# Left halves of the adjacency cast by GpSimd's transfers, the attention row spread by TensorE, ScalarE's table loaded first, and new ranks, in a two-layer graph kernel

## The chip, the core and the metric

The kernel runs on one core of a Trainium2 chip. The core has five engines that run their own instruction streams in program order: TensorE (PE, matrix products into PSUM), VectorE (DVE), ScalarE (ACT), GpSimd (POOL) and SyncE (SP). SP, ACT and POOL also issue transfers; 16 DMA engines carry them. The metric is the device time of the program in microseconds, as the median of several runs.

## The reference

There are 16 graphs of 1024 nodes with 128 features, `x`, and one 0/1 adjacency matrix `adj` of 1024 x 1024 for all of them. Layer 0 is an attention layer, layer 1 a gated graph network of five steps; each is followed by a residual sum and a layer norm.

```python
# layer 0
h = x @ others_weight
u1, u2 = h @ a1, h @ a2                      # att_weight, two halves of 128
e = u1[:, idx1] + u2[:, idx2]                # idx1, idx2: fixed pairs (2m, 2m+1) mod n
e = where(e >= 0, e, 0.1 * e)
att = softmax(where(adj > 0, e, -9e15), axis=1)
x = layernorm(x + att @ h + x @ self_weight)
# layer 1
for _ in range(5):
    m = adj @ h                              # used twice: in_matrix = out_matrix = adj
    av = concatenate([m, m])
    u3 = h @ u3_w.T + u3_b
    z = sigmoid(av @ w3_w.T + w3_b + u3)
    r = sigmoid(av @ w4_w.T + w4_b + u3)
    hv = tanh(av @ w5_w.T + w5_b + (r * h) @ u5_w.T + u5_b)
    h = (1 - z) * h + z * hv
x = layernorm(x + h)
```

Because of the fixed pairs, the logits of the left 512 columns of `adj` depend on a pair of neighbouring nodes only, and those of the right 512 columns on the row alone. So the kernel treats the two halves of `adj` apart: for the left half it needs weighted row sums (the softmax's denominators), for the right half a plain count of ones in each row.

## The kernel before

**Tables.** `adj` (transposed by the host) is kept in SBUF for the whole run as `adj`, eight chunks c of 128 rows by 1024 columns, of type float32r, the type of the message products. float32 comes from memory, and a conversion has to write the float32r: the transfers land in staging tiles (`staged[k][e]`, chunk pair k = 0 to 3, e = 0 the left 512 columns, e = 1 the right), and `adj_tables` converts. The right halves go through ScalarE, which counts the ones as it copies (L497, `cnt`). The left halves are plain copies (L494), by VectorE for c < 4 and by ScalarE for the rest.

**Order.** All work is handed to `Plan` as operations with an engine, an assumed length in ns, a rank (lower is more urgent), and what they read and write. `Plan.order()` runs a list schedule over these assumed lengths and emits each engine's instructions in the order that comes out. On the chip the engines keep that order and wait on semaphores for the data. `rank_of(b, s)` gives graph b's step s its rank, from `D["q"]`, `D["s"]` and a correction in `NUDGE`; the constants of `D` shift single kinds of operation (`r`, `hv`, `tr`, `pr` of the gates, `l1` to `l8` the parts of layer 0, with own values for graphs 0 and 1). `lands(...)` are made-up operations on an engine "DMA" which tell the plan when a load is thought to arrive.

**The first microseconds.** `early_loads` (L347) issues, from SP and ACT by turns: graph 0's `x` in two halves, `others_weight`, the attention weights copied to all 128 partitions by the transfer itself (L351), the eight staged pieces of `adj`, `self_weight`, and graph 1's `x`. `ahead` (L461) then has SP load further graphs' `x` (L468). `constants` (L400, GpSimd) writes the identity matrix `ident` and the small tiles `shift`, `ones` and `mhalf`. `late_loads` (L378) makes GpSimd wait for the last staged piece before it issues the gates' weights.

TensorE begins with two `fill_` matmuls of the identity (L440) and then, wherever the plan finds no useful work for it, up to `IDLE` = 60 pairs of idle transposes of the identity (L436); nothing reads their results. Meanwhile VectorE's `wv_` (L412) multiplies `others_weight` by the two halves of the attention row, and sums (L414, L423). The result, in `T_ws` and `wo`, is what TensorE needs for graph 0's `spread_` (L767: the logit row of graph 0, spread to all partitions) and for the products `ph` (L690).

Graph 0's exponentials follow on VectorE and ScalarE (L770 to L783, into `pb`), then eight row sums `z_` (L855, VectorE), one for each chunk's left half, which for graph 0 read the staging tile; the reciprocals `rz_` (L874 to L878); the split of the scaled `h` into a high and a low float32r half, `hi_` on ScalarE (L907) and `lo_` on VectorE (L913); and the products `po` with `adj` (L648, with `po`). From there on TensorE works on several graphs at once: layer 0 of later graphs (`ph`, `po`, `px`) fits between the steps of layer 1, whose messages are the other products of L648 and whose gates are L1234, L1244, L1260 and L1261. The products `px` of graphs 4 to 7 (L472) can be done at any time and have a rank just before the idle transposes.

Of the kernel before, what the change touches and what calls it, by code (L numbers as in the profile page):

```python
# [17 lines left out]
P = 128  # L18
# [17 lines left out]
IDLE = 60  # L36
NUDGE = {(3, 2): -0.6, (3, 3): 0.3, (0, 1): -0.5, (1, 1): 0.45, (2, 3): -0.2, (3, 1): -1.2, (3, 0): 0.6, (0, 2): 0.25, (2, 2): -0.6, (1, 4): -1.2, (1, 3): 0.3, (0, 3): -0.6, (1, 2): -0.15, (4, 0): -0.1, (2, 0): 1.2, (2, 1): 0.05, (4, 4): -0.3, (2, 4): -0.15, (7, 3): -0.75, (5, 4): 1.2, (4, 3): 1.25, (6, 3): -1.5, (6, 4): -0.6, (8, 2): 0.15, 10: 0.05, (11, 3): -1.2, (11, 4): 0.3, (7, 2): 0.3, (8, 3): -0.6, (12, 3): -0.45, (13, 3): -0.9, (12, 0): 1.15, (10, 3): -0.35, (8, 4): 0.05, (12, 4): -0.3, (12, 1): -0.05, (11, 2): -0.15, 12: -0.05, (13, 4): 1.2, (13, 0): 1.2, (11, 1): 0.05, (12, 2): 0.15, (10, 4): 0.1, (15, 0): -0.6, (14, 2): -0.6}
# [106 lines left out]
def kernel(  # L144
# [79 lines left out]
    def exact(pools):  # L224
# [84 lines left out]
        D = dict(m=-0.05, pu=1.4, u=0.95, pr=0.55, pz=0.85, r=0.25, pv=1.05, z=1.3, hv=-0.7, h=1.2, tr=2.55, o=6.35, ln=2.5, out=4.4, l1=-9, l2=-4, l3=-2, l4=-5.5, l5=-7.25)  # L309
        D.update(l6=-1.35, l7=-1, l8=-2, q=10, s=4.2, even=1, base=-1, q1=-6, b1=4, lz=-4, l1_0=-9, l2_0=-4, lz_0=-4, l3_0=-2, l4_0=-4, l5_0=-7, l6_0=-1.5, l7_0=-1, l8_0=-2)  # L310
        D.update(l1_1=-10, l2_1=-9, lz_1=-4, l3_1=-2, l4_1=-4, l5_1=-7, l6_1=-1.5, l7_1=-1, l8_1=-2, tab=8, tabc=1, cl=-5.9, ca=-50, cr=-51, px=-3.5, own=-2, ownw=-4.6)

# [22 lines left out]
        def W(name):  # L335
            return T(boot)[:, cols[name]]

        ws = ("T", "ws")
        staged = [[("blk", "boot", k, e) for e in range(2)] for k in range(NC // 2)]
        x0 = ("xt", 0)  # L340

        def adj_half(k, e):
            hs = slice(e * HALF, (e + 1) * HALF)
            rows = adj_t[2 * k * P : 2 * (k + 1) * P, hs].rearrange("(c p) n -> p c n", p=P)
            return T(staged[k][e], F32, [P, 2, HALF]), rows

        def early_loads():  # L347
            nc.sync.dma_start(T(x0)[:, HALF:N], x_t[0][:, HALF:N])
            nc.scalar.dma_start(T(x0)[:, 0:HALF], x_t[0][:, 0:HALF])
            nc.sync.dma_start(wo[:, 0:P], others_w)  # L350
            nc.scalar.dma_start(T(ws)[:, P : 3 * P], att_w.rearrange("k o -> o k").to_broadcast([P, 2 * P]))  # L351
            nc.sync.dma_start(*adj_half(0, 0))
            nc.scalar.dma_start(*adj_half(1, 0))
            nc.sync.dma_start(*adj_half(0, 1))
            nc.scalar.dma_start(*adj_half(1, 1))
            nc.sync.dma_start(W("ws"), self_w)
            for k in range(2, NC // 2):
                for e in range(2):
                    nc.sync.dma_start(*adj_half(k, e))
            nc.sync.dma_start(T(("xt", 1)), x_t[1])  # L360
# [5 lines left out]
            writes=[(boot, "early"), (ws, "early"), (x0, "early"), (("xt", 1), "early"), *((t, "early") for k in staged for t in k)],  # L366
# [5 lines left out]
        lands(4700, [(x0, 0), (x0, 1)])  # L372
        lands(400, [(("wo",), 0), (ws, "att")])
        for ns, k, e in ((3600, 0, 0), (1400, 1, 0), (1000, 0, 1), (1400, 1, 1), (1600, 2, 0), (1400, 2, 1), (1400, 3, 0), (1400, 3, 1)):
            lands(ns, [(staged[k][e], 0), *([(boot, "ws")] if (k, e) == (2, 0) else [])])
        lands(1400, [(("xt", 1), 0), (("xt", 1), 1)])

        def late_loads():  # L378
            nc.gpsimd.tensor_copy(mark, T(staged[3][1])[0:1, 0, 0:1])
# [15 lines left out]
            reads=[(staged[3][1], 0)],  # L395
# [4 lines left out]
        def constants():  # L400
            make_identity(nc, ident)
            nc.gpsimd.memset(shift, -SHIFT)
            nc.gpsimd.memset(ones, 1.0)
            nc.gpsimd.memset(mhalf, -0.5)

        plan.add("POOL", 1400, -100, constants, writes=[(("ident",), 0), (("ones",), 0)])


        def column_(t, cols, n):
            nc.tensor.transpose(T(t)[:, 0:n], T(ws)[0:n, cols], ident[0:n, 0:n])  # L410

        def wv_():  # L412
            for two in range(2):
# [4 lines left out]
                    T(ws)[:, (1 + two) * P : (2 + two) * P],  # L418
# [12 lines left out]
        dve(650, -101, wv_, reads=[(ws, "att"), (("wo",), 0)], writes=[(ws, 0), (("look", "wv"), 0)])  # L431
# [58 lines left out]
        def adj_tables(c):  # L490
            st = staged[c // 2]

            def left(copy):
                copy(adj[:, c, 0:HALF], T(st[0])[:, c % 2])  # L494

            def right():
                nc.scalar.activation(adj[:, c, HALF:N], T(st[1])[:, c % 2], AF.Identity, accum_out=cnt[:, c : c + 1])  # L497

            if c < 4:
                dve(420, D["cl"], lambda: left(nc.vector.tensor_copy), reads=[(st[0], 0)], writes=[(("A",), c, 0)])  # L500
            else:
                act(A, D["ca"], lambda: left(nc.scalar.copy), reads=[(st[0], 0)], writes=[(("A",), c, 0)])
            act(640, D["cr"], right, reads=[(st[1], 0)], writes=[(("A",), c, 1)])

        def quarter(i, j):
# [1235 lines left out]
```

## Time and profile before

| | |
|---|---|
| Median of 9 runs | 1455.59 us (1453.86 to 1457.94) |
| Profiled execution, its own time | 1456.06 us |
| Its span, first to last instruction | 1454.5 us |
| Granted TensorE clock, mean over the span | 0.996 |
| Instructions | 17779 |
| Idle transposes (L436) | 120, 14.3 us busy |
| Fill matmuls (L440) | 4 passes, 3.7 us busy |
| Left-half casts (L494) | 4 on VectorE, 1.6 us; 4 on ScalarE, 2.4 us |
| Right-half copies (L497) | 8, 5.0 us, and 1.8 us for reading their sums |
| DMA of the span | 174.28 MB, mean 120 GB/s |

The span is the time from the first to the last instruction of one profiled execution; the program's own time lies 1.6 us above it. Busy shares are of the span. TensorE's busy time counts idle transposes and fills too. The profile gives a float32 matmul as two passes (`x4` for two matmuls), and matmuls overlap, so that the length of one in a row is longer than the time from one to the next. In the timeline the lines "SPq", "ACTq" and "POOL ... DMA_DIRECT2D" are issues of transfers, the time that the issuing engine needs for them, not the transfers.

### The profile page before, as it was taken

The numbers are of one execution on the slowest core, as the hardware profiler recorded it, in microseconds if no ns is written. First come the engines' busy times: TensorE is split into PE (matmuls) and PEld (weight loads), VectorE is DVE, ScalarE is ACT, GpSimd is POOL, SyncE is SP. The second block draws the span as 40 slices with busy tenths as digits, with TensorE's granted clock in tenths as the row PEclk, the third lists the DMA queues.
The fourth block names the chain that finished last, engine by engine and source line by source line (L and its number), as shares of the span: only waits on it lengthen the run. The fifth ranks groups of instructions, "written<-read, shape, count | busy, mean of one in ns | idle before, by whom it ended". The sixth has DMA issues, their size and how long they took to land. (4 is left out here: it accounts for less than half of the span.)

```text
span 1454.5 us, 17779 instructions
## 1 busy us (share of the span) xinstructions
PE 1435.8 (99%) x5017; PEld 899.2 (62%) x5017; DVE 1160.3 (80%) x2752; ACT 898.2 (62%) x1793; POOL 192.1 (13%) x334
## 2 busy tenths in 40 slices
PE   9999999999999999999999999999999999999996
PEld 7666666566666666666656556666665666566562
DVE  6886989879888798888889698887988876865635
ACT  5665546656656766576656666566574766653644
POOL 1221001102010120111101121010210112000302
PEclk9999999999999999999999999999999999999998
DMA  8245135544344643364445543365423554223111
GB/s 289 89 132 148 56 109 164 156 136 125 83 135 129 178 136 102 97 179 130 117 114 147 152 124 81 103 172 161 120 76 94 153 160 113 75 66 87 37 37 32
DMA packets 187299, 174.28 MB, mean 120 GB/s; under 512 B 34408, under 2 KB 136504, under 8 KB 187192
## 3 DMA queue, kind: packets, MB, share of 16 engines
q1 hardware_dynamic: 180920, 155.23, 37.8%
q0 software_dynamic: 5168, 16.26, 3.4%
q10 hardware_dynamic: 1104, 1.57, 0.3%
q8 instruction: 41, 0.67, 0.2%
q14 instruction: 66, 0.54, 0.1%
HBM read 95.74 MB, written 77.24 MB: 119 GB/s over the span
## 5 line engine op out<-in xcount | busy, mean ns | idle before, releaser
L1261 PE MATMUL ps_g_v<-r,u5h 128*128 128x512 f32 x320 | 163.5, 592 | 0.5 <-DVE r L1254 0.5
L1260 PE MATMUL ps_g_v<-m,wm 128*128 128x512 f32 x320 | 163.4, 592 | 0.0
L1254 DVE SCALAR_TENSOR_TENSOR r<-r,hT 128x512 f32<-128x512 f32 x160 | 109.1, 686 | 64.0 <-ACT r L1247 63.2
L1244 PE MATMUL ps_g_r<-m,wm 128*128 128x512 f32 x320 | 159.1, 593 | 1.0 <-ACT gz L1237 1.0
L1244 PE MATMUL gz<-m,wm 128*128 128x512 f32 x320 | 158.1, 592 | 0.0
L1269 DVE TENSOR_TENSOR hv<-hv,hT 128x512 f32<-128x512 f32 x160 | 109.8, 686 | 55.2 <-ACT hv L1266 54.4
L1234 PE MATMUL ps_g_r<-hT,u 128*128 128x512 f32 x320 | 152.7, 592 | 0.0
L1247 ACT ACTIVATE r<-ps_g_r,bh 128x512 f32<-128x512 f32 x160 | 109.3, 686 | 64.4 <-PE ps_g_r L1244 63.7
L648 PE MATMUL ps_acc_a<-tab,blk_s 128*128 128x512 f32 x544 | 147.7, 413 | 0.0
L648 PE MATMUL ps_acc_po<-adj,blk 128*128 128x512 f32 x512 | 139.6, 418 | 0.1
L1237 ACT COPY gz<-ps_g_r 128x512 f32<-128x512 f32 x160 | 91.3, 572 | 63.2 <-PE ps_g_r L1234 61.8
L648 PEld LDWEIGHTS ps_acc_a<-tab,blk_s 128*128 128x128 f32 x544 | 101.1, 188 | 33.3 <-issue 8.1
L1247 ACT ACTIVATE z<-gz,bh 128x512 f32<-128x512 f32 x160 | 109.5, 687 | 17.7 <-PE gz L1244 17.2
L648 PEld LDWEIGHTS ps_acc_po<-adj,blk 128*128 128x128 f32 x512 | 95.8, 188 | 35.1 <-issue 11.5
L1275 DVE SCALAR_TENSOR_TENSOR hT<-hv,hT 128x512 f32<-128x512 f32 x160 | 108.4, 680 | 1.5
L1272 DVE SCALAR_TENSOR_TENSOR hv<-z,hv 128x512 f32<-128x512 f32 x160 | 108.3, 678 | 0.6
L1261 PEld LDWEIGHTS ps_g_v<-r,u5h 128*128 128x128 f32 x320 | 60.6, 190 | 77.5 <-issue 61.3
L1244 PEld LDWEIGHTS gz<-m,wm 128*128 128x128 f32 x320 | 60.3, 189 | 74.8 <-issue 74.3
L606 DVE STREAM_TRANSPOSE T<-hT 128x512 f32<-128x512 f32 x138 | 95.5, 700 | 3.9 <-DMA X<-T 3.2
L648 PE MATMUL ps_acc<-adj,blk_h 128*128 128x512 f32 x384 | 95.4, 402 | 1.0 <-ACT blk_h L636 0.8
L1260 PEld LDWEIGHTS ps_g_v<-m,wm 128*128 128x128 f32 x320 | 60.0, 190 | 57.6 <-issue 51.7
L640 DVE TENSOR_TENSOR blk_s<-G,blk_s 128x512 fp32r<-128x512 f32 x136 | 91.8, 680 | 2.9 <-ACT blk_s L636 2.7
(199 smaller groups left out, 2520.8 us busy)
## 6 DMA issues: line engine op xcount, KB each, us to landing
G<-X SPq DMA_DIRECT2D x140, 256.0 KB, 2.9
X<-T SPq DMA_DIRECT2D x552, 64.0 KB, 1.8
yd<-y POOLq DMA_DIRECT2D x32, 256.0 KB, 3.1
D_y<-T_y SPq DMA_DIRECT2D x112, 64.0 KB, 1.9
F_y<-D_y SPq DMA_DIRECT2D x28, 256.0 KB, 2.8
X<-y SPq DMA_DIRECT2D x28, 256.0 KB, 2.1
D_b<-T_b SPq DMA_DIRECT2D x112, 64.0 KB, 2.6
F_b<-D_b SPq DMA_DIRECT2D x28, 256.0 KB, 2.9
```

What stands on the lines that cost most here:

```text
L606: nc.vector.transpose(T(t).rearrange("p (b c i) -> p b c i", b=4, c=4), turned(src()))
L640: lambda: nc.vector.tensor_tensor(half(1), src(), half(0), ALU.subtract),
L648: nc.tensor.matmul(T(bank), T(blk)[:, k, c, :], right(c), start=(first and i == 0), stop=(last and i == len(terms) - 1), skip_group_check= ...
L1234: nc.tensor.matmul(T(pr), u3, h(), start=True, stop=True)
L1244: nc.tensor.matmul(T(p_), wm[:, j, :], T(m), start=False, stop=True, skip_group_check=True)
L1247: nc.scalar.activation(T(t), T(p_), AF.Tanh, bias=bh[:, j : j + 1], scale=0.5 * sg)
L1254: lambda r=r, h=h: nc.vector.scalar_tensor_tensor(T(r), T(r), 1.0, h(), ALU.add, ALU.mult),
L1260: nc.tensor.matmul(T(pv), wm[:, 2, :], T(m), start=True, stop=False)
L1261: nc.tensor.matmul(T(pv), u5h, T(r), start=False, stop=True)
L1269: nc.vector.tensor_tensor(T(hv), T(hv), h(), ALU.subtract)
L1272: nc.vector.scalar_tensor_tensor(T(hv), T(z), 1.0, T(hv), ALU.add, ALU.mult)
L1275: nc.vector.scalar_tensor_tensor(h(), T(hv), 0.5, h(), ALU.mult, ALU.add)
```

## The change

- `early_loads` no longer loads the left halves of `adj`; the staging tiles for them are gone. SP issues the four right halves; ACT issues only its half of `x` and the attention weights, now as one row on one partition.
- `constants` issues four transfers from GpSimd, one for each chunk pair, from `adj` in memory straight into the left half of the float32r table; the transfer converts. They stand after the memsets of `ones` and `shift`, and before the identity and `mhalf`. Its assumed length in the plan is 1400 ns, as before.
- The eight left-half copies of `adj_tables` are gone. The row sums `z_` of graph 0 read the table.
- `pw_` is a new TensorE operation: a matmul with a row of ones copies the attention row to all partitions, in PSUM, and `wv_` reads it there.
- `first_` is a new ScalarE operation at the head of its queue: an exponential of one element, which makes it the first operation to use ScalarE's table.
- The assumed arrivals (`lands`) are new, `IDLE` is 48, and a part of the ranks in `D` and `NUDGE` has other values.

```diff
--- before.py
+++ after.py
@@ -33,8 +33,8 @@
 AHEAD = range(4, 8)
 LATE = 3001
 TURNED = {(0, 0), (0, 1), (7, 2), (7, 3)}
-IDLE = 60
-NUDGE = {(3, 2): -0.6, (3, 3): 0.3, (0, 1): -0.5, (1, 1): 0.45, ...}
+IDLE = 48
+NUDGE = {(3, 2): -0.75, (3, 3): 0.75, (0, 1): -0.5, (1, 1): 1.05, ...}
 
 
 class Plan:
@@ -306,9 +306,9 @@
             plan.add("SP", *a, **k)
 
 
-        D = dict(m=-0.05, pu=1.4, u=0.95, pr=0.55, pz=0.85, r=0.25, pv=1.05, z=1.3, hv=-0.7, h=1.2, tr=2.55, o=6.35, ln=2.5, out=4.4, l1=-9, l2=-4, l3=-2, l4=-5.5, l5=-7.25)
-        D.update(l6=-1.35, l7=-1, l8=-2, q=10, s=4.2, even=1, base=-1, q1=-6, b1=4, lz=-4, l1_0=-9, l2_0=-4, lz_0=-4, l3_0=-2, l4_0=-4, l5_0=-7, l6_0=-1.5, l7_0=-1, l8_0=-2)
-        D.update(l1_1=-10, l2_1=-9, lz_1=-4, l3_1=-2, l4_1=-4, l5_1=-7, l6_1=-1.5, l7_1=-1, l8_1=-2, tab=8, tabc=1, cl=-5.9, ca=-50, cr=-51, px=-3.5, own=-2, ownw=-4.6)
+        D = dict(m=-0.05, pu=1.4, u=0.95, pr=0.75, pz=0.85, r=0.45, pv=1.05, z=1.3, hv=0.3, h=1.2, tr=2.35, o=6.35, ln=2.5, out=4.4, l1=-9, l2=-5, l3=-2, l4=-4.5, l5=-7.25)
+        D.update(l6=-1.35, l7=-2, l8=-2.4, q=10, s=4.2, even=1, base=-1, q1=-6, b1=4, lz=-5, l1_0=-7, l2_0=-4, lz_0=-4, l3_0=0, l4_0=-4, l5_0=-7, l6_0=-0.5, l7_0=-5, l8_0=-4)
+        D.update(l1_1=-12, l2_1=-8, lz_1=-3, l3_1=-2, l4_1=-6, l5_1=-7, l6_1=-2.5, l7_1=-2, l8_1=-2, tab=8, tabc=1.5, cl=-5.9, ca=-50, cr=-51, px=-4.0, own=-2, ownw=-4.6)
 
         def on_pe(b, what):
 
@@ -336,47 +336,45 @@
             return T(boot)[:, cols[name]]
 
         ws = ("T", "ws")
-        staged = [[("blk", "boot", k, e) for e in range(2)] for k in range(NC // 2)]
+        staged = [("blk", "boot", k) for k in range(NC // 2)]
         x0 = ("xt", 0)
 
-        def adj_half(k, e):
-            hs = slice(e * HALF, (e + 1) * HALF)
-            rows = adj_t[2 * k * P : 2 * (k + 1) * P, hs].rearrange("(c p) n -> p c n", p=P)
-            return T(staged[k][e], F32, [P, 2, HALF]), rows
+        def adj_rows(k, e):
+            return adj_t[2 * k * P : 2 * (k + 1) * P, e * HALF : (e + 1) * HALF].rearrange("(c p) n -> p c n", p=P)
+
+        def adj_half(k):
+            return T(staged[k], F32, [P, 2, HALF]), adj_rows(k, 1)
 
         def early_loads():
             nc.sync.dma_start(T(x0)[:, HALF:N], x_t[0][:, HALF:N])
             nc.scalar.dma_start(T(x0)[:, 0:HALF], x_t[0][:, 0:HALF])
+            nc.scalar.dma_start(T(ws)[0:1, P : 3 * P], att_w.rearrange("k o -> o k"))
             nc.sync.dma_start(wo[:, 0:P], others_w)
-            nc.scalar.dma_start(T(ws)[:, P : 3 * P], att_w.rearrange("k o -> o k").to_broadcast([P, 2 * P]))
-            nc.sync.dma_start(*adj_half(0, 0))
-            nc.scalar.dma_start(*adj_half(1, 0))
-            nc.sync.dma_start(*adj_half(0, 1))
-            nc.scalar.dma_start(*adj_half(1, 1))
-            nc.sync.dma_start(W("ws"), self_w)
-            for k in range(2, NC // 2):
-                for e in range(2):
-                    nc.sync.dma_start(*adj_half(k, e))
+            for k in range(NC // 2):
+                nc.sync.dma_start(*adj_half(k))
+                if k == 1:
+                    nc.sync.dma_start(W("ws"), self_w)
             nc.sync.dma_start(T(("xt", 1)), x_t[1])
 
         sp(
             9500,
             -103,
             early_loads,
-            writes=[(boot, "early"), (ws, "early"), (x0, "early"), (("xt", 1), "early"), *((t, "early") for k in staged for t in k)],
+            writes=[(boot, "early"), (ws, "early"), (x0, "early"), (("xt", 1), "early"), *((t, "early") for t in staged)],
         )
 
         def lands(ns, what):
             plan.add("DMA", ns, -103, lambda: None, writes=what, lag=0)
 
-        lands(4700, [(x0, 0), (x0, 1)])
-        lands(400, [(("wo",), 0), (ws, "att")])
-        for ns, k, e in ((3600, 0, 0), (1400, 1, 0), (1000, 0, 1), (1400, 1, 1), (1600, 2, 0), (1400, 2, 1), (1400, 3, 0), (1400, 3, 1)):
-            lands(ns, [(staged[k][e], 0), *([(boot, "ws")] if (k, e) == (2, 0) else [])])
+        lands(4650, [(x0, 0), (x0, 1), (ws, "att")])
+        lands(650, [(("wo",), 0)])
+        for ns, k, e in ((2000, 0, 0), (1400, 0, 1), (1400, 1, 0), (1400, 1, 1), (1600, 2, 0), (1400, 2, 1), (1400, 3, 0), (1400, 3, 1)):
+            landed = [(staged[k], 0)] if e else [(("A",), c, 0) for c in (2 * k, 2 * k + 1)]
+            lands(ns, landed + ([(boot, "ws")] if (k, e) == (2, 0) else []))
         lands(1400, [(("xt", 1), 0), (("xt", 1), 1)])
 
         def late_loads():
-            nc.gpsimd.tensor_copy(mark, T(staged[3][1])[0:1, 0, 0:1])
+            nc.gpsimd.tensor_copy(mark, T(staged[3])[0:1, 0, 0:1])
             for j, w in enumerate((w3_t, w4_t, w5_t)):
                 nc.gpsimd.dma_start(
                     W("w345")[:, 256 * j : 256 * (j + 1)].rearrange("p (t e) -> p t e", t=2),
@@ -392,22 +390,34 @@
             11000,
             -80,
             late_loads,
-            reads=[(staged[3][1], 0)],
+            reads=[(staged[3], 0)],
             writes=[(boot, "late"), (("uw",), 0), (ws, "b")],
             lag=2500,
         )
 
         def constants():
+            nc.gpsimd.memset(ones, 1.0)
+            nc.gpsimd.memset(shift, -SHIFT)
+            for k in range(NC // 2):
+                nc.gpsimd.dma_start(adj[:, 2 * k : 2 * k + 2, 0:HALF], adj_rows(k, 0))
             make_identity(nc, ident)
-            nc.gpsimd.memset(shift, -SHIFT)
-            nc.gpsimd.memset(ones, 1.0)
             nc.gpsimd.memset(mhalf, -0.5)
 
         plan.add("POOL", 1400, -100, constants, writes=[(("ident",), 0), (("ones",), 0)])
+
+        def first_():
+            nc.scalar.activation(mark, shift[0:1, :], AF.Exp)
+
+        act(1600, -104, first_, reads=[], writes=[(("mark",), 0)])
 
 
         def column_(t, cols, n):
             nc.tensor.transpose(T(t)[:, 0:n], T(ws)[0:n, cols], ident[0:n, 0:n])
+
+        pw = ("ps", "g", "w")
+
+        def pw_():
+            nc.tensor.matmul(T(pw)[:, 0 : 2 * P], ones[0:1, 0:1].to_broadcast([1, P]), T(ws)[0:1, P : 3 * P], start=True, stop=True)
 
         def wv_():
             for two in range(2):
@@ -415,7 +425,7 @@
                     T(("look", "wv"))[:, two * P : (two + 1) * P],
                     wo[:, 0:P],
                     1.0,
-                    T(ws)[:, (1 + two) * P : (2 + two) * P],
+                    T(pw)[:, two * P : (two + 1) * P],
                     ALU.mult,
                     ALU.mult,
                     accum_out=wv[:, two : two + 1],
@@ -428,7 +438,8 @@
             nc.vector.tensor_copy(wo[:, P : P + 2], wv)
             nc.vector.tensor_copy(wo[:, P + 2 : P + 3], T(ws)[:, 0:1])
 
-        dve(650, -101, wv_, reads=[(ws, "att"), (("wo",), 0)], writes=[(ws, 0), (("look", "wv"), 0)])
+        pe(450, -101, pw_, reads=[(ws, "att"), (("ones",), 0)], writes=[(pw, 0)])
+        dve(750, -101, wv_, reads=[(pw, 0), (("wo",), 0)], writes=[(ws, 0), (("look", "wv"), 0)], lag=-250)
         dve(190, -65, wo_, reads=[(ws, 0)], writes=[(("wo",), 1)])
 
         def idle_():
@@ -490,19 +501,10 @@
         def adj_tables(c):
             st = staged[c // 2]
 
-            def left(copy):
-                copy(adj[:, c, 0:HALF], T(st[0])[:, c % 2])
-
             def right():
-                nc.scalar.activation(adj[:, c, HALF:N], T(st[1])[:, c % 2], AF.Identity, accum_out=cnt[:, c : c + 1])
-
-            if c < 4:
-                dve(420, D["cl"], lambda: left(nc.vector.tensor_copy), reads=[(st[0], 0)], writes=[(("A",), c, 0)])
-            else:
-                act(A, D["ca"], lambda: left(nc.scalar.copy), reads=[(st[0], 0)], writes=[(("A",), c, 0)])
-            act(640, D["cr"], right, reads=[(st[1], 0)], writes=[(("A",), c, 1)])
-
-
+                nc.scalar.activation(adj[:, c, HALF:N], T(st)[:, c % 2], AF.Identity, accum_out=cnt[:, c : c + 1])
+
+            act(640, D["cr"], right, reads=[(st, 0)], writes=[(("A",), c, 1)])
 
         def quarter(i, j):
             return lambda c: adj[:, 4 * i + c, j * HALF : (j + 1) * HALF]
@@ -849,12 +851,10 @@
             rank = rank0(b) + lv("lz")
             for c in range(NC):
 
-                st = staged[c // 2][0]
-
-                def z_(c=c, st=st):
+                def z_(c=c):
                     nc.vector.scalar_tensor_tensor(
                         T(junk),
-                        T(st)[:, c % 2] if b == 0 else adj[:, c, 0:HALF].bitcast(F32),
+                        adj[:, c, 0:HALF].bitcast(F32),
                         1.0,
                         pairs()[:, c // 4, :],
                         ALU.mult,
@@ -862,7 +862,7 @@
                         accum_out=T(zs)[:, c : c + 1],
                     )
 
-                entries = (st, 0) if b == 0 else (("A",), c, 0)
+                entries = (("A",), c, 0)
                 dve(740, rank, z_, reads=[(pb, 0), (pb, 1), entries], writes=[(zs, c), (junk, 0)])
 
 
```

(`NUDGE` is cut: it also has new values for other steps of graphs 0 to 3, and three new entries; those of graphs 4 to 15 are unchanged.)

## The prediction

> **What bounds the kernel.** I read the page's busy shares first, then TensorE's waits, then the first 30 us of the timeline, then GpSimd's rows there.
>
> ```profile
> PE 1435.8 (99%) x5017; PEld 899.2 (62%) x5017; DVE 1160.3 (80%) x2752; ACT 898.2 (62%) x1793; POOL 192.1 (13%) x334
> ```
>
> TensorE is busy in all but 18.7 us of the 1454.5 us span. Its waits over the whole span (us in total, times, longest):
>
> ```profile
> PE ps_t L598 <- DVE hT L1275: 4.4, 2, 3.6
> PE gz_fill L440 <- POOL ones L403: 1.4, 1, 1.4
> PE ps_g_r L1244 <- ACT gz L1237: 1.0, 2, 0.7
> PE ps_acc L648 <- ACT blk_h L636: 0.8, 1, 0.8
> PE ps_g_v L1261 <- DVE r L1254: 0.5, 1, 0.5
> PE ps_acc L648 <- DVE blk_h L640: 0.2, 1, 0.2
> PE ps_t_b L598 <- ACT y L565: 0.2, 1, 0.2
> ```
>
> These are 8.5 us; the other 10 us lie behind the last transposes of the tail. In the middle TensorE goes from one useful matmul to the next, so it can't be shortened there. The change keeps every useful matmul and adds one. So I count TensorE's **waste**: the wait before its first matmul, the fills of L440, the idle transposes of L436, the waits. What the waste loses, the end gains, one for one. The head of the timeline holds most of it (start, length, engine, line, what; in brackets the idle time before it):
>
> ```profile
> 1.35 3.68 PE L440 MATMUL gz_fill<-ident 128*128 128x512 f32 x4 [1.35 <-POOL ones L403]
> 4.87 3.44 PE L436 MATMUL ps_idle<-ident 128*128 128x128 f32 x30
> 7.16 0.29 DVE L414 SCALAR_TENSOR_TENSOR look_wv<-wo,T_ws 128x128 f32<-128x128 f32 x1 [7.16 <-DMA T_ws<-in_L_gnn_att_weight_dram]
> 8.14 1.90 PE L767 MATMUL ps_p<-xt,T_ws 128*128 128x512 f32 x4
> 10.13 1.28 ACT L779 ACT_TABLE_LOAD   x1 [10.13 <-PE ps_p L767]
> 11.66 4.75 PE L436 MATMUL ps_idle<-ident 128*128 128x128 f32 x42
> ```
>
> TensorE runs in program order. The fills need the identity, cost 3.5 us (1.35 to 4.87: these first passes are slow, 0.86 us against the 0.43 of L767's), then idle transposes at 4.68/42 = 0.11 us each cover the wait for the attention row.
>
> **GpSimd's queue, the dear part.** `constants` now issues four casting transfers ahead of the identity. What one issue holds GpSimd for, from its rows:
>
> ```profile
> 1.29 0.10 POOL L403 MEMSET ones<- 128x2 f32 x1
> 19.86 2.41 POOL L381 DMA_DIRECT2D hT_boot<-in_L_gnn_w_w_dram  x3
> 22.26 0.58 POOL L385 DMA_DIRECT2D u<-in_L_gnn_u_w_dram  x1
> 26.56 0.49 POOL L388 DMA_DIRECT2D T_ws<-in_L_gnn_u_b_dram  x1 [1.71 <-DMA hT_boot<-in_L_gnn_w_w_dram]
> 44.64 0.66 POOL L1054 DMA_DIRECT2D yd<-y  x1 [2.86 <-ACT y L565]
> ```
>
> One row costs 0.49, 128 rows 0.58 (64 KB) or 0.66 (256 KB), 256 rows 0.80. No row casts. The new transfers have 256 rows of 2 KB, so the nearest is 0.80. Lower end 0.49; upper end 2.1, if the cast cuts each row into four pieces of 512 bytes (768 more rows, at 0.22 per 128, from the step 0.58 to 0.80). I take 0.80: 4 x 0.80 = 3.2 us. The identity (0.2 and 0.29) follows, so TensorE starts at about 4.6 instead of 1.35: **+3.2** (ends +2.0 and +8.4). Behind the transfers wait only the identity, mhalf, and the late loads, which waited until 19.73 for adj anyway. `ones` and `shift` go ahead, so the row's matmul and the table load don't wait for the transfers themselves; but in TensorE's queue the row's matmul stands behind fills and idle transposes, so it is late with them.
>
> The Trainium skill weighs against 0.80 here: "DMA: Bandwidth & Descriptors", on the anatomy of a DMA of the GpSimd path, puts the dispatch at about 50 ns and the making of descriptors at "small, variable". By it four issues would be some 0.2 us, an estimate, and the sum would end near -2.1 instead of +0.9; the 0.80 of this trace decides.
>
> **IDLE from 60 to 48**: 24 transposes fewer, 24 x 0.11 = **-2.7**. They have to be replaced by useful work, or TensorE merely waits in their place; that is a rival below.
>
> **The attention row**: one matmul of 256 columns, two passes at half of L767's 0.43: **+0.43**, with VectorE's sums behind it (some 0.2 us of draining; 0.9 for L414 and L423), which the idle transposes planned between them cover. The broadcast load goes. With it the first spread would be free of the 7.16, but TensorE now gets there later: start 4.6, fills to 8.1, about 14 transposes to 9.7, the row to 10.1, sums to 11.2. The spread stands at some 11.3 instead of 8.14. That the row lands early is worth nothing, hidden by TensorE's own queue.
>
> **Table load first**: 1.28 us leave the chain spread, exponentials, row sums, and go where ScalarE waited until 10.13. **Casts gone**: four of 0.42 on VectorE, four of 0.62 on ScalarE (2.5). ScalarE worked without pause from 10.13 to the first L907 at 23.79, 13.7 us; less 1.28 and 2.5 it is 9.9, from 11.3 + 2.0 = 13.3 to 23.2. VectorE's last reciprocals, before at 22.7, come at about 22.7 + 3.2 - 1.3 - 0.4 = 24.2. So the split halves for the first products are ready about when they were (24.2 against 23.8), while TensorE reaches them 0.9 late: no new wait, and no gain either. All of this costs and brings nothing on TensorE's count; without the slack it would cost the 0.4.
>
> **Transfers.** In us 4 to 6 the DMA engines moved 83 GB/s, in 6 to 20 385. Without the dip 2 x (385 - 83) = 0.6 MB come earlier, 1.6 us, so adj would be there at 18.1 rather than 19.7. Two fewer issues on ScalarE's queue, two fewer on SP's: each 0.4 to 0.5, all before either engine has other work, so nothing. Row sums now wait for the cast tile instead of the staged one; same landing. The cast's rate is in no row: bounds are the 385 of the plain loads and half of it (below).
>
> **New ranks**: best, all waits that aren't the last one of the tail go: 1.0 + 0.8 + 0.5 + 0.2 + 0.2 + 0.8 (4.4 - 3.6) = -3.5. Worst, each of the eight pairs gets a hole like that at 40 to 50 us, where TensorE was busy 8.8 of 10: +9.7. I take 0, since the middle is already full.
>
> **Sum**: 3.2 - 2.7 + 0.43 = **+0.9** on the profiled span of 1454.5. That execution took 1456.06, 0.5 over the median of 1455.59; I add to the median: **1456.5**.
>
> **Rivals.**
> B, the waits go: the new ranks and earlier loads take away all 3.5 us: 0.9 - 3.5 = -2.6, 1453.0; with issues at 0.49 it is 2.0 - 2.7 + 0.4 - 3.5 = -3.8, 1451.8. For it: fewer fillers are asked for. Against: TensorE starts later, and the waits near 46 to 50 follow a chain over GpSimd's row statistics that no edit shortens.
> C, the issues are dear (slower): place, GpSimd's first microseconds; price 4 x issue - 2.3; it decides from 1.3 us an issue, where the sum is +2.9. At 2.1 it is +6.1, 1461.7. For: no cast in the trace. Against: all three kinds of issue lie below 0.81.
> D, the casting transfers move at half rate (slower): 2.1 MB take 10.8 us instead of 5.4, adj is there at 23.5, 3.8 later than before, TensorE only 0.9 later; it stands 2.9, where the dropped transposes were: +3.8, 1459.4. It decides from about two thirds of the rate on.
> E, the ranks open holes in the middle: up to +9.7; two such holes, 2.4, make +3.3, 1458.9.
> That the change doesn't do what it says, casting elsewhere, I see no way to.
>
> **How the numbers follow.** What a measurement of this kernel can tell from no change is about 0.2%, 2.9 us: faster is below 1452.7, slower above 1458.5. Forecast 0.50 (its own range 1454.5 to 1459: issues of 0.7 to 1.0, a wait more or less; 0.03 of it slower), B 0.20 (0.18 faster, since it needs nearly all its waits or a cheap issue; 0.02 same), C 0.13, D 0.10, E 0.07. So faster 0.18, same 0.49, slower 0.33. The range 1452 to 1461 leaves out B's far part and the far parts of C and E.
>
> **What would show it.** GpSimd's four issues between the memsets and the identity, their length, and TensorE's first matmul at 4 to 5 us; the spread at 11 rather than 8; 96 idle transposes; the table load before 3.5 us; no casts at L494; waits of TensorE before 50 us no longer than before. An issue below 0.5 or above 1.3 us, a fresh wait of 2 us between 15 and 35 us, or holes in the middle would make me wrong.

## The result, and the profile after

The changed kernel takes 1461.52 us (median of 9 runs, 1458.68 to 1463.42), beside 1455.30 us for the kernel before on the same chip (29 runs, 1453.71 to 1457.94). The ratio is 1.004, interval 1.0032 to 1.0048: 6.2 us slower, where +0.9 was forecast and 1461 was the upper end. The profiled execution took 1459.51 us, its span is 1457.7 us, 3.2 more than before; it is one of the quicker of its kind, so only half of the loss can be read in it. A further 0.25 of the loss lies outside the span: the program's own time is 1.56 above it before and 1.81 after.

Busy time and instruction counts of the page, and TensorE's waits (us in total, times, longest):

```profile
PE 1434.1 (98%) x4995; PEld 897.7 (62%) x4995; DVE 1158.6 (79%) x2748; ACT 898.3 (62%) x1790; POOL 210.2 (14%) x338
```

```profile
PE gz_fill L451 <- POOL mhalf L404: 5.0, 1, 5.0
PE ps_t L600 <- DVE hT L1275: 4.4, 2, 3.6
PE ps_acc_a L650 <- ACT m L1186: 1.9, 1, 1.9
PE ps_g_r L1244 <- ACT gz L1237: 1.2, 1, 1.2
PE ps_acc_c L650 <- DVE blk_s L642: 0.8, 1, 0.8
PE ps_acc L650 <- DVE blk_h L642: 0.5, 1, 0.5
```

TensorE has 22 passes fewer (24 idle transposes less, two passes of the row more). The wait at the end of the tail is the same 3.6. The wait for the identity grew from 1.4 to 5.0. And there are new rows in the middle: single waits of up to 1.9 us on products there, where the largest was 0.8.

The head of the timeline (start, length, engine, line, what; in brackets the idle time before it):

```profile
1.31 3.10 POOL L402 DMA_DIRECT2D adj<-in_adj_dram  x4 [0.45 <-issue]
1.76 1.28 ACT L409 ACT_TABLE_LOAD   x1 [1.76 <-issue]
...
5.05 3.48 PE L451 MATMUL gz_fill<-ident 128*128 128x512 f32 x4 [5.05 <-POOL mhalf L404]
8.36 1.69 PE L447 MATMUL ps_idle<-ident 128*128 128x128 f32 x14
9.98 0.69 PE L420 MATMUL ps_g_w<-T_ws,ones 1*128 1x256 f32 x2
10.71 0.29 DVE L424 SCALAR_TENSOR_TENSOR look_wv<-wo,ps_g_w 128x128 f32<-128x128 f32 x1 [10.71 <-PE ps_g_w L420]
11.75 1.88 PE L769 MATMUL ps_p<-xt,T_ws 128*128 128x512 f32 x4
```

Four issues hold GpSimd from 1.31 to 4.41, 0.775 us each. The identity follows, and TensorE's first matmul is at 5.05. The row's matmul, its sums and the spread come as a chain behind that.

The middle has the new part. First the timeline near 360 us, then TensorE, TensorE's weight loads, VectorE, ScalarE and GpSimd in stretches of 2 us (busy us and instructions of each, then granted clock, DMA share, GB/s):

```profile
358.52 0.34 SPq L626 DMA_DIRECT2D G<-X  x1
359.04 1.50 PE L692 MATMUL ps_g_ph<-wo,xt 128*128 128x131 f32 x12
361.28 0.62 ACT L638 CAST blk_x<-G 128x512 fp32r<-128x512 f32 x1 [4.50 <-DMA G<-X]
361.80 0.58 ACT L1186 COPY m<-ps_acc_a 128x512 f32<-128x512 f32 x1
362.44 3.26 PE L650 MATMUL ps_acc_a<-tab,blk_s 128*128 128x512 f32 x8 [1.89 <-ACT m L1186]
```

```profile
360.00:362.00 2.00, 0.55 (x5) 0.35 (x4) 0.07 (x1) 0.72 (x2) 0.00 (x0) 1.00 0.84 256
362.00:364.00 2.00, 1.56 (x5) 1.28 (x6) 2.00 (x5) 1.22 (x4) 0.00 (x0) 0.77 0.44 118
364.00:366.00 2.00, 2.00 (x7) 1.61 (x7) 1.65 (x4) 0.26 (x1) 0.00 (x0) 0.50 0.20 51
366.00:368.00 2.00, 2.00 (x9) 1.39 (x9) 1.64 (x9) 1.22 (x3) 0.00 (x0) 0.88 0.63 107
```

In ScalarE's program the cast of a message block (L638) stands ahead of the copy that frees TensorE's accumulator (L1186). The cast waits for a transfer that was issued at 358.52; ScalarE stands idle for 4.50 us, and the copy, whose input had been there since about 359.2, stands behind it. TensorE waits 1.89 us for the copy, then runs for 3.41 us at half the clock (363.07 to 366.49 in the records), which loses about 1.7 more.

Summing, over the whole span, the gaps between the starts of successive matmuls beyond their regular step (worked out from the two traces), together with what the granted clock did at the start and at the end, gives this account of the profiled 3.2 us:

| | before | after | difference, us |
|---|---|---|---|
| wait for the first matmul | 1.35 | 5.05 | +3.7 |
| idle transposes | 120 | 96 | -2.6 |
| the fills, at half speed | 3.5 us | 3.3 us | -0.2 |
| the row's matmul | | | +0.5 |
| holes behind the head, half clock included | about 5 | about 7 | about +2 |
| the tail: the last 40 matmul passes, to the end | 27.6 us | 26.7 us | -0.9 |
| sum | | | about +2.5 |

The after column's 7 are 0.7 at 51 us, 2.05 and 1.7 at 360, 1.4 at 549 and 1.2 at 646. The rows miss the 3.2 by 0.7, so they are good to no better than that. The tail's term isn't the change's doing: in both traces the granted clock falls to 0.50 near the end, 12.7 us ahead of it in the one and 9.2 in the other, and traces of runs below that keep the order of before have 26.6 us there too (cast_late) and 27.7 (table_only).

### The profile page after: what moved, and what is told of

Same layout as the page of the kernel before. It is cut to its first block, busy times and chain, and to the rows that moved or that the text cites. A ratio compares the mean times of both kernels' runs of the same rounds, so it can differ in the third digit from the quotient of the medians.

```text
span 1457.7 us, 17706 instructions
## 1 busy us (share of the span) xinstructions
PE 1434.1 (98%) x4995; PEld 897.7 (62%) x4995; DVE 1158.6 (79%) x2748; ACT 898.3 (62%) x1790; POOL 210.2 (14%) x338
## 5 line engine op out<-in xcount | busy, mean ns | idle before, releaser
L650 PE MATMUL ps_acc<-adj,blk_h 128*128 128x512 f32 x384 | 98.6, 408 | 0.5 <-DVE blk_h L642 0.5
L638 ACT CAST blk_s<-G 128x512 fp32r<-128x512 f32 x136 | 82.5, 617 | 25.3 <-DVE G L1128 23.1
```

Of the source, the lines that this page charges most:

```text
L650: nc.tensor.matmul(T(bank), T(blk)[:, k, c, :], right(c), start=(first and i == 0), stop=(last and i == len(terms) - 1), skip_group_check= ...
```

## The experiments

The theory: two things cost time, GpSimd's four issues ahead of the identity, and holes of another planned order. Rivals: that the holes come only from the late start; that the casting transfers or the missing broadcast are to blame; that the new ranks alone make the loss. In each run below the kernel before was timed beside it, at 1455.65 to 1455.76 us (19 to 33 runs); ratios are to it. A difference of 1 us or less between the medians of two changed kernels is within the scatter.

**ident_first**: the changed kernel with the identity made before the four issues; every engine's order is otherwise that of the changed kernel.

```diff
             nc.gpsimd.memset(shift, -SHIFT)
+            make_identity(nc, ident)
             for k in range(NC // 2):
...
-            make_identity(nc, ident)
```

> The changed kernel with the identity written ahead of GpSimd's four transfers; every engine's order of work is otherwise that of the changed kernel. Theory 1 (late start plus holes from the new ranks): TensorE's first matmul at 1.7 us instead of 5.04, its spread at some 8.4 instead of 11.75, 3.4 us off the time, the waits of the middle stay: 1461.5 - 3.4 = 1458.1. Rival 2 (the holes in the middle come from the late start, which puts the engines out of step with the planned order): both go, 3.4 + 4.6: 1453.5. Rival 3 (the row sums are what sets the head, TensorE only waits elsewhere): no change, 1461.5, with new waits of TensorE before 35 us.

Measured: 1456.53 us (1455.57 to 1459.19), ratio 1.001 (1.0001 to 1.0019), 5.0 less than the changed kernel. Its head in the timeline, and two of its waits:

```profile
1.42 3.78 PE L451 MATMUL gz_fill<-ident 128*128 128x512 f32 x4 [1.42 <-POOL ident masks.py:199]
...
1.51 3.12 POOL L403 DMA_DIRECT2D adj<-in_adj_dram  x4
...
4.99 2.95 PE L447 MATMUL ps_idle<-ident 128*128 128x128 f32 x14
...
7.87 0.69 PE L420 MATMUL ps_g_w<-T_ws,ones 1*128 1x256 f32 x2
```

```profile
PE ps_acc_a L650 <- ACT m L1186: 1.7, 1, 1.7
...
PE ps_g_r L1244 <- ACT gz L1237: 1.2, 1, 1.2
```

TensorE starts 3.6 earlier, and the holes are the same two instructions with nearly the same lengths (1.7 and 1.2, after 1.9 and 1.2): they belong to the order, not to the late start. This trace has no stretch at half clock between its head and its tail. The time fell by 1.6 more than the 3.4 that were expected. And the spread starts at 9.65, where 8.4 was expected: the 14 idle transposes ahead of the row's matmul took 2.95 us, one in 0.21 until 7.55 and in 0.11 from there on, where the changed kernel's took 1.69. The row's matmul follows the last of them at once, so it doesn't wait for its row.

**ranks_only**: the kernel before with the new ranks and IDLE 48, nothing else.

```diff
-IDLE = 60
+IDLE = 48
...
-        D = dict(m=-0.05, pu=1.4, u=0.95, pr=0.55, ... r=0.25, ... hv=-0.7, ...)
+        D = dict(m=-0.05, pu=1.4, u=0.95, pr=0.75, ... r=0.45, ... hv=0.3, ...)
...
```

> The kernel before with only the new ranks and IDLE = 48; transfers, casts, table and row as before. Theory 1: 24 idle transposes fewer, -2.6, and the holes of the new ranks, +4.6: 1455.3 - 2.6 + 4.6 = 1457.3. Rival 2 (holes from the late start): -2.6 alone, 1452.7. Rival 4 (all of the loss is the ranks'): 1461.5.

Measured: 1459.18 us (1457.56 to 1460.51), ratio 1.0022 (1.0012 to 1.0032), 3.5 slower, though it too has 24 idle transposes fewer. Its trace has holes at 43 to 46 us (2.2), 51 (1.9), 775 (1.45) and around 1250 (two, 1.9 in sum). The first isn't new, since before has as much at 46 to 50; the others are.

**old_ranks**: the reverse, the changed kernel with the ranks and IDLE of before.

```diff
-IDLE = 48
+IDLE = 60
...
-        D = dict(m=-0.05, pu=1.4, u=0.95, pr=0.75, ... r=0.45, ... hv=0.3, ...)
+        D = dict(m=-0.05, pu=1.4, u=0.95, pr=0.55, ... r=0.25, ... hv=-0.7, ...)
...
```

> The changed kernel with the ranks and IDLE = 60 of the kernel before; the new transfers, row and table stay. Theory 1: start +3.7, row's matmul +0.5, no fewer fillers, no holes from ranks: 1455.3 + 4.2 = 1459.5. Rival 2: holes too, 1464. Rival 4: 1455.3 to 1456.

Measured: 1464.33 us (1463.18 to 1465.52), ratio 1.0058 (1.0044 to 1.0072). That is the 1464 of rival 2, and 4.8 over what the theory gave. It is worse than the changed kernel by 2.8, of which the 24 more idle transposes, at 0.11 each, can be 2.6. So the new ranks alone aren't to blame: the changed operations lose as much under the old ones. Which ranks fit them better isn't shown. Its windows, with the columns as above:

```profile
50.00:52.00 2.00, 0.65 (x5) 0.29 (x2) 1.86 (x9) 1.36 (x4) 0.68 (x1) 1.00 0.59 229
52.00:54.00 2.00, 0.66 (x2) 0.48 (x2) 1.86 (x9) 2.00 (x8) 0.18 (x1) 0.73 0.05 18
54.00:56.00 2.00, 2.00 (x6) 1.52 (x6) 2.00 (x8) 2.00 (x8) 0.37 (x1) 0.50 0.34 131
56.00:58.00 2.00, 2.00 (x9) 1.60 (x8) 2.00 (x7) 0.61 (x3) 0.00 (x0) 0.50 0.00 0
58.00:60.00 2.00, 2.00 (x7) 1.57 (x6) 1.23 (x5) 2.00 (x7) 0.00 (x0) 0.57 0.00 0
```

TensorE is idle for 2.7 of the first 4 us, in two waits; they are followed by 6.83 us at half clock, exactly twice 3.41. Together they cost 2.7 + 3.4 = 6.1. Whether the late start has a part in these two waits isn't settled, as no run has the old ranks with the identity first; cast_late, below, has the late start in before's own order, and no wait there beyond before's 0.8.

**row_table**: the kernel before with the row's matmul and the first exponential as new operations; old ranks, IDLE 60, and the casts stay.

```diff
-            nc.scalar.dma_start(T(ws)[:, P : 3 * P], att_w.rearrange("k o -> o k").to_broadcast([P, 2 * P]))
+            nc.scalar.dma_start(T(ws)[0:1, P : 3 * P], att_w.rearrange("k o -> o k"))
...
+        act(1600, -104, first_, reads=[], writes=[(("mark",), 0)])
...
+        pe(450, -101, pw_, reads=[(ws, "att"), (("ones",), 0)], writes=[(pw, 0)])
...
```

> The kernel before with only the row spread by TensorE and ScalarE's table loaded first; the casts, the staged halves, the ranks and 60 idle pairs stay. Theory 1 (in the head TensorE's own queue of fills and idle transposes sets the pace, so an earlier row and table only lengthen the slack of the others): 1455.3 + 0.5 = 1455.8, spread within 0.5 us of 8.14. Rival 5 (the chain row, exponentials, sums sets the head): the row lands some 2 us earlier and the table's 1.3 us go, 1452 to 1454.

Measured: 1468.64 us (1465.94 to 1469.42), ratio 1.0082 (1.0069 to 1.0096): 13 us slower, the expectation missed by 13. Some 1.2 of them lie outside the span, which the program's own time exceeds by 2.5 to 2.9 here and by 1.6 in before. The spread stands at 9.69, where it was expected within 0.5 of 8.14: 18 idle transposes, the row's matmul and 10 more idle transposes stand ahead of it. Its longest middle waits of TensorE:

```profile
PE ps_g_r L1256 <- ACT gz L1249: 3.0, 4, 2.1
PE gz L660 <- ACT gz L1198: 2.1, 1, 2.1
PE ps_acc_po L660 <- ACT hv L1278: 1.4, 1, 1.4
PE ps_acc_c L660 <- DVE m L1208: 1.4, 1, 1.4
```

None of these rows has to do with the row or the table. Two operations in the first 10 us, and another assumed length for `wv_`, give the list schedule another state, and another order comes out for the whole program; this one has holes at 105, 550 to 600, 882 and 1130 us, the last with 3.41 us of half clock behind it. So a part of the change can't be measured by adding its operations to the plan. The kernels that follow therefore keep an order as it is: that of before, or that of ident_first.

**cast_after**: before's own order; the casting transfers issued behind the identity, the eight casts and the loads of the staged left halves gone.

```diff
-            nc.sync.dma_start(*adj_half(0, 0))
-            nc.scalar.dma_start(*adj_half(1, 0))
...
             make_identity(nc, ident)
...
+            for k in range(NC // 2):
+                rows = adj_t[2 * k * P : 2 * (k + 1) * P, 0:HALF].rearrange("(c p) n -> p c n", p=P)
+                nc.gpsimd.dma_start(adj[:, 2 * k : 2 * k + 2, 0:HALF], rows)
...
-                copy(adj[:, c, 0:HALF], T(st[0])[:, c % 2])
+                pass
```

> The kernel before, in its own planned order on every engine, with GpSimd's four casting transfers (behind the identity) in place of the staged left halves and their eight casts; nothing else. Theory 1 (casts and landings are hidden in the head, and holes come only with another order): 1455.5, within 1 us, the holes of the middle as before. Rival 6 (the casting transfers bring holes by themselves, late or in contention): over 1458. Rival 7 (the eight casts were on the path): 1453 or less.

Measured: 1455.05 us (1454.01 to 1456.09), ratio 0.9996 (0.9987 to 1.0005): the same time. The casting transfers, the new landings and the eight missing casts are worth nothing, as forecast.

**cast_late**: the same, with the four issues ahead of the identity.

```diff
-            make_identity(nc, ident)
...
                 nc.gpsimd.dma_start(adj[:, 2 * k : 2 * k + 2, 0:HALF], rows)
+            make_identity(nc, ident)
```

> As the kernel with the casting transfers in the old order, but with the four issues ahead of the identity, as in the change. Theory 1: TensorE's first matmul at 5.0 instead of 1.4, and since its order is fixed, 3.6 us more: 1459.1. Rival 2 (a late TensorE also breaks the planned order and opens holes further on): 1461 or more. Rival 8 (the later waits at 45 to 50 us shrink by what TensorE is late): 1456 to 1457.

Measured: 1458.50 us (1457.26 to 1459.07), ratio 1.0022 (1.0012 to 1.0031). Against cast_after, 3.45 us. TensorE's waits, first of cast_after, then of cast_late:

```profile
PE gz_fill L440 <- POOL ones L400: 1.4, 1, 1.4
PE ps_acc L648 <- ACT blk_h L636: 0.8, 1, 0.8
```

```profile
PE gz_fill L440 <- POOL mhalf L404: 5.0, 1, 5.0
...
PE ps_acc L648 <- ACT blk_h L636: 0.8, 1, 0.8
```

Of the rows over 0.2 us only the first differs, by 3.6. This is the price of the four issues in front of the identity, with nothing else mixed in.

**table_only**: before's order with one early exponential.

```diff
             nc.gpsimd.memset(shift, -SHIFT)
+            nc.scalar.activation(mark, shift[0:1, :], AF.Exp)
             nc.gpsimd.memset(ones, 1.0)
```

> The kernel before, in its own order, with one exponential of a single element early on ScalarE, so that the table is loaded before 4 us and not at 10.13. Theory 1 (hidden: TensorE's idle transposes run past the exponentials anyway): 1455.5. Rival 5 (the chain from the spread over the exponentials to the row sums sets the head): 1.3 less, 1454.2.

Measured: 1456.27 us (1455.17 to 1457.38), ratio 1.0004 (0.9995 to 1.0013). The timeline has the load early, and ScalarE then waits for TensorE:

```profile
2.69 1.28 ACT L403 ACT_TABLE_LOAD   x1 [2.69 <-issue]
...
10.81 0.69 ACT L780 ACTIVATE pb<-ps_p,shift 128x512 f32<-128x512 f32 x1 [6.62 <-PE ps_p L768]
```

The exponentials start at once when their input comes, and the time is the same: hidden, as forecast.

**thin**: ident_first without the 20 idle transposes ahead of graph 1's `ph`.

```diff
-            for j in range(2):
+            idles.append(0)
+            for j in range(0 if 34 <= len(idles) <= 43 else 2):
```

> The kernel with the identity first, with the 20 idle transposes ahead of graph 1's products (22.06 in the changed kernel) left out of TensorE's stream; every other instruction stays in its place. Theory 1 (idle transposes hold up work whose data is there): 20 x 0.11 = 2.2 us less than that kernel, 1454.3. Rival 9 (they only cover a wait for data): unchanged, 1456.5, with a wait of TensorE of 2 us before 30 us.

Measured: 1457.44 us (1454.62 to 1460.5), ratio 1.0014 (1.0005 to 1.0023), where 2.2 less than ident_first was expected; it took 0.9 more. Its waits:

```profile
PE ps_acc_a L653 <- ACT m L1189: 2.6, 1, 2.6
...
PE ps_acc L653 <- DVE blk_h L645: 1.2, 1, 1.2
```

In this trace TensorE gives back a part of what it gains in the head where it waits for something else: the wait at 360 us grew from 1.7 to 2.6, since TensorE came 1.2 us earlier and the transfer in front of it only 0.34 (issued at 356.32, in ident_first at 356.66). This 2.6 us wait was not followed by a lower clock. But the trace is that of thin's quickest execution (1454.62 us). For every run its mean granted clock is on record: it is 0.994 or 0.995 in eight of thin's eleven runs and in one of ident_first's. One stretch of 3.41 us at 0.50 takes 0.0012 off this mean. So most of thin's executions had more time at half clock, some 2.0 us on the average of the two kernels' clocks (0.9951 and 0.9965; an estimate from them), and that is about what the 20 transposes should have brought.

**swap**: ident_first with one ScalarE instruction moved, the copy L1186 near 358 us ahead of the cast that waits for the transfer.

```diff
-            for i in plan.order():
+            started = plan.order()
...
+            late = copies[27]
+            cast = acts[acts.index(late) - 1]
+            started.remove(late)
+            started.insert(started.index(cast), late)
+            for i in started:
```

> The kernel with the identity first, with one ScalarE instruction moved: the copy of the message m that TensorE waited 1.7 to 1.9 us for near 360 us (L1186) goes ahead of the conversion blk_x (L638), which stood in front of it in ScalarE's queue and waited for a load. Theory 1 (that hole is the new order's doing, at this one place): the hole goes, 1.9 us and more in runs where the clock falls with it, 1454.5. Rival 10 (the hole only moves to the next wait): 1456.5.

Measured: 1455.57 us (1453.89 to 1458.23), ratio 1.0 (0.9991 to 1.0009), 1.0 less than ident_first and between the 1454.5 of the theory and the 1456.5 of rival 10. The timeline there:

```profile
356.19 0.59 ACT L1186 COPY m<-ps_acc_a 128x512 f32<-128x512 f32 x1 [2.76 <-PE ps_acc_a L650]
357.25 2.11 PE L650 MATMUL ps_acc_a<-tab,blk_s 128*128 128x512 f32 x8
357.81 0.62 ACT L638 CAST blk_x<-G 128x512 fp32r<-128x512 f32 x1 [1.04 <-DMA G<-X]
```

TensorE's row has no bracket any more: the hole is gone, so its cause is shown. What it is worth in time isn't: the two intervals overlap. In the trace a wait of 1.6 us near 771 has come up that ident_first's doesn't have, again for a copy at L1186, which this time stands in ScalarE's queue behind an instruction that waits for GpSimd (L567).

**row_first**: ident_first with the attention row issued ahead of half of `x` on ScalarE's queue.

```diff
-            nc.scalar.dma_start(T(x0)[:, 0:HALF], x_t[0][:, 0:HALF])
             nc.scalar.dma_start(T(ws)[0:1, P : 3 * P], att_w.rearrange("k o -> o k"))
+            nc.scalar.dma_start(T(x0)[:, 0:HALF], x_t[0][:, 0:HALF])
```

> The kernel with the identity first, with ScalarE's two first loads swapped: the attention row of 1 KB ahead of the half of x. TensorE there reached the row's matmul at 6.6 us and began it at 7.87. Theory 1 (the row is late because it is queued behind the half of x): 1.3 us less, 1455.2, the row's matmul before 6.8 us. Rival 11 (a small load lands late wherever it stands, or the row isn't the last to come): no change, 1456.5.

Measured: 1458.44 us (1455.7 to 1459.15), ratio 1.0017 (1.0007 to 1.0026). The row's matmul stands at 6.88 and the spread at 8.65, each 1.0 earlier. That isn't the row's doing, as the heads of two timelines show, this one's and that of swap, whose loads have ident_first's order:

```profile
5.00 1.95 PE L447 MATMUL ps_idle<-ident 128*128 128x128 f32 x14
6.88 0.69 PE L420 MATMUL ps_g_w<-T_ws,ones 1*128 1x256 f32 x2
```

```profile
4.71 1.69 PE L447 MATMUL ps_idle<-ident 128*128 128x128 f32 x14
6.33 0.69 PE L420 MATMUL ps_g_w<-T_ws,ones 1*128 1x256 f32 x2
```

In swap the row was there by 6.33, without first place in the queue. In all three the row's matmul starts 0.2 us after the start of the last idle transpose; what differs is how long these run at 0.21 us each instead of 0.11: in ident_first until 7.55, here until about 5.5, in swap not at all. So the 6.6 at which TensorE was taken to reach the row's matmul in ident_first was a misreading, and this experiment says nothing on when the row lands. The median rose by 1.9. In the profiled execution (1456.15 us) the hole at 360 us is followed by 3.41 us at half clock, which ident_first's profile didn't have. Of the eleven times two lie at 1455.7 and 1456.15, the others at 1457.7 to 1459.15. More time at half clock doesn't explain this upper group: the mean granted clock on record is 0.996 for the two quick runs, and for the others 0.995 to 0.997, with 0.997 for three of them. What does explain it stays open.

**cast_thin** and **cast_thin2**: cast_after, so the order of before, without the last 10 and the last 16 of the 60 idle pairs.

```diff
-            for j in range(2):
+            idles.append(0)
+            for j in range(0 if len(idles) >= 51 else 2):
```

> The kernel with the casting transfers in the old order and the identity first, without the last ten pairs of idle transposes (24 to 30 us). Theory 1 (their data is there): 20 x 0.11 = 2.2 us less, 1452.9. Rival 9 (they cover waits, or the holes at 46 to 50 us grow by as much): 1455.

> As the last, without the last 16 pairs (from 21 us on). Theory 1: 32 x 0.11 = 3.5 us less than with all of them, 1451.6. Rival 9: 1453 to 1455, with waits before graph 1's products (22.3 us) or a larger hole at 46 to 50 us.

Measured: 1453.31 us (1452.5 to 1456.73), ratio 0.9986 (0.9977 to 0.9995); and, with 45 in place of 51, 1453.12 us (1450.9 to 1454.92), ratio 0.9982 (0.9973 to 0.9991). The first 20 transposes bring 1.7 of 2.2 us, the next 12 only 0.2 of 1.3, which is within the scatter. Four of cast_thin2's waits bear on that:

```profile
PE ps_g_r L1247 <- ACT gz L1240: 0.6, 1, 0.6
PE ps_g_r L1247 <- DVE m L1199: 0.5, 1, 0.5
PE ps_p L802 <- ACT u L717: 0.4, 1, 0.4
PE ps_pairs L820 <- DVE u L710: 0.3, 1, 0.3
```

The last two are at 24 and 25 us: TensorE now waits where it idled. The first two are further on, at 1000 and 657 us; at 657 cast_thin waits 1.3. cast_thin2 beats both kernels: 2.6 us under the one before, 8.4 under the changed one, with the change's casting transfers and fewer idle transposes, and without its new order.

## Why the prediction was wrong

**GpSimd's issues: right.** 0.80 each was forecast from the nearest row, 0.775 measured. The start is at 5.05, not 4.6, since the first issue came only at 1.31, behind 0.45 us in which GpSimd stood idle after the memsets. The term of +3.2 measured +3.7 in the profile, and +3.45 in time (cast_late against cast_after). In the new order moving the identity is worth 5.0 rather than 3.45; no trace shows where the other 1.5 lie; the stretch at half clock, about 1.7, is in the changed kernel's profile and not in that of ident_first. For the rule of the Trainium skill that was weighed ("DMA: Bandwidth & Descriptors", the anatomy of a transfer on the GpSimd path: the dispatch at some 50 ns, the making of descriptors "small, variable"), these four issues of 0.775 us are the measurement, and it decides.

**IDLE: right as a count, -2.6 for -2.7**, 96 transposes in the profile. But that they count one for one was nearly true for the last 20 in the order of before (cast_thin, 1.7 of 2.2), and not in the new order (thin: none in the median, whose runs have lower mean clocks on record).

**The row's matmul: +0.5 for +0.43; the spread at 11.75 for 11.3.** That an early row is worth nothing held, and for the forecast's reason, TensorE's own queue: the row was there by 6.33 in swap, and in every trace with this operation its matmul starts as soon as the idle transposes ahead of it are through (9.98 in the changed kernel).

**Table, casts, transfers: 0, right.** table_only 1.0004, cast_after 0.9996, both intervals with 1 inside. Rivals C (0.775 is far from 1.3 us an issue) and D (adj isn't late: cast_after has no wait that before doesn't have) fall. Rival B falls too: none of the new order's traces has fewer waits than before.

**The step that failed** is "New ranks", and its words "I take 0, since the middle is already full". That TensorE's middle is full was nearly true of the order that had been profiled (its largest holes between 60 us and the tail are 0.7 to 0.9, at 285, 312 and 1002 us); the ranks make another order, about which that profile says nothing. Holes of the new ranks were the bound that I had named (up to +9.7), and rival E's mechanism, two holes for +3.3, with a chance of 0.07. Set against the forecast's own terms, 3.2 - 2.7 + 0.43 = +0.9, the measured +6.2 leaves 5.3 us, of which 0.7 are the mis-sized head. The rest, some 4.6, is the term that was put at 0. It is a remainder, not a measurement: the profiled execution shows about 2 of it as holes and half clock, and idle transposes that bring nothing in this order (thin) may be a part of it. By ident_first some 3.0 of it are there with an early start too (0.9 over before, where -2.6 and +0.5 were to come), and the other 1.5 only with the late one. ranks_only has the same term without the head: +3.5 where -2.7 was to come, a remainder of 6.2, of which its trace shows some 5 as new holes.

So the mechanism of rival E is shown: by ident_first (same instructions wait, whatever the start), by swap (one instruction moved, its hole gone; the time it is worth not clear of noise) and by ranks_only, old_ranks and row_table (each another order, each with other holes, +3.5 to +13). Left open: which of the new ranks put the cast ahead of the copy, which wasn't tried, and how the remainder divides. Half clock is not all of it: among the changed kernel's runs on record the one of 1462.08 us has a mean granted clock of 0.997, the one of 1460.01 has 0.995.

## What to carry to other kernels

Where a list schedule over assumed lengths writes the order, an added operation or rank can replace the whole order; measure the idea with the old order kept, and only then let the plan run anew. Look in the new order for an instruction that waits for a transfer in front of one that frees another engine's buffer. And what an issuing engine does first is paid by everyone who waits for its next instruction: here four issues in front of the identity cost 3.45 us in the order of before, and behind it nothing.

## What the hardware did that was not expected

A wait of 1.89 us of TensorE was followed by 3.41 us at a granted clock of 0.50, and two waits of 2.7 us in sum by 6.83 us; other waits, of 1.7 us (ident_first) and even 2.6 us (thin), by none. So the price of a hole isn't its length alone. The Trainium skill ("TensorE: Matmul & The Clock Gate", part 1) tells of a free-running window of 3413 ns, at half speed after an idle one. The length of the steps agrees; a TensorE that stands idle for a whole window is ahead of none of these stretches, where it had waited for 2.1 us at most at a time.

The traces show more of the pattern. Within a trace all changes of the granted clock lie whole steps of 3.413 us apart: in the changed kernel's they are at 8.09, 363.07, 366.49 and 1448.51, which is 104, 1 and 317 steps. In the middle of the traces a stretch at 0.50 begins where TensorE had no matmul for 1.78 to 2.11 us of the step before (the changed kernel 1.89, row_first 1.78, old_ranks 2.07, row_table 2.11), and none where it was 1.63 or less (swap). thin's 2.6 us fall on two steps, 0.97 and 1.58. The bound isn't sharp, since 1.98 us in a step of row_first's tail had no such stretch behind it, and old_ranks' second stretch follows 0.62. At the start it is the same steps: matmuls run at half speed until one of them ends, which is at 4.4 us in swap and at 7.6 in ident_first, though TensorE begins at 1.42 in both. So two single profiles can differ by 1 us or more in the head, and by 0.9 in the tail, for this reason alone.

A 1 KB row onto one partition was there by 6.33 us (swap), where its copies onto 128 partitions, issued from the same place in the queue, had landed at 7.16 in before, 6.94 in cast_thin2 and 7.42 in table_only. And transfers that convert float32 to float32r cost nothing that the time shows (cast_after, ratio 0.9996).
